# Sixteen more groups through the dense path of a one-core GNN attention kernel, and another order of the dense work within a batch

## The chip, the cores and the metric

One core of a Trainium2 chip runs the whole kernel. The metric is the device time in microseconds of one execution; three runs of the kernel before gave 3377.53 us in the median (3377.07 to 3377.69). The profile was taken in a separate execution that took 3376.22 us. A measurement of this kernel can tell a difference of about 0.2% from no change.

The engines are named as in the profile: PE is TensorE's matmul, PEld its weight load, DVE is VectorE, ACT is ScalarE, POOL is GpSimd and SP is SyncE, whose queue issues most DMAs.

## The reference, cut to what matters

12,500 nodes with 64 features; 400,000 edges with 64 features, sorted by destination. The density of the destinations falls with the node's number (they are drawn as 12500 u^2), so the first nodes have many edges each and the last ones few.

```python
h_src = nfeats[src]; h_dst = nfeats[dst]
e = leaky_relu(concat([h_src, h_dst, efeats]) @ W_attn + b_attn)[:, 0]
m = concat([h_src, efeats]) @ W_ne
alpha = segment softmax of e over dst
z = segment_sum(alpha[:, None] * m, dst)
out = relu(concat([nfeats, z]) @ W_out)
x = layernorm(x + out)
```

## The kernel before

Edges are cut into 782 groups of 512 (128 partitions by 4 places). There are two ways for a group.

**Gathered groups.** For each group four indirect DMAs on POOL (`gather`, L330) fetch 128 rows of 65 numbers from a table in DRAM: the node's score and its 64 features. 662 groups go this way, that is 2648 gathers. Sixteen groups make a batch and four make a part of a batch, so a batch has 64 gathers and four parts; there are 43 batches (numbered from 0), the last four of them smaller (10, 10, 12 and 6 groups, `ENDS`). A part gets its scores on DVE (`scores`, L373 to L391; the step L380 adds the gathered score and so waits for the gathers; ACT copies the window row and the edge rows first, L370 and L371). When all four parts have scores, a softmax over segments follows (`softmax`), which begins with the transpose L692 and ends with the transpose L754. It hops between DVE, ACT and PE four times: the first scan, line rows on PE (L596 `lines<-ident,bnd`), ends on one row, back to columns on PE (L599 `lines<-ident,line`), and the same again for the sums. The four gaps between these hops are filled by `dense_step(0)` to `dense_step(3)`. After the softmax the weights are made (L789), then PE multiplies the parts (L806): parts 0 and 1 at once, parts 2 and 3 ("later") in the gaps of the next batch's softmax. I call these products p0 to p3.

**Dense groups.** The first 120 groups, with the densest nodes, are not gathered. Each costs, spread over many batches:

- a *lookup* of its node scores: ACT makes a one-hot tile in a `big` buffer (L430, L431), PE multiplies it (L441), DVE picks the score (`look_scores`, L466 to L472). `look_rows` (L451 to L460) adds the edges' part, once a batch;
- after the softmax of its round (12 groups), a *count*: ACT makes four one-hot tiles (L480, L481) and one or two more where a group spans 6 or 7 nodes (L493, L494), DVE makes the weighted `lows` (L483), PE multiplies (L488, and L496 for the extra nodes), DVE adds the result into `counts` (`dense_sum`, L506, L509);
- *edge products* on PE (L549) and their sum on DVE (`edge_sum`, L558);
- per chunk of groups, a *node product* of `counts` with all node features: 25 matmuls on PE (L565). Then `node_pick` on DVE (L573, L576, and L578, which clears `counts`), `node_turn` on PE (L584) and `node_sum` on DVE (L590). I call a batch with a node product a node batch.

There are six `big` buffers, and each is free again only when PE has multiplied it. The dense groups are looked up and counted four per batch up to group 84 and three per batch beyond. Their chunks are 36, 12, 12, 8, 8, 8 groups and then six of 6, so that in the tail a node product comes with every second batch.

All engines run in the order in which the program is written (`manual_schedule`), each queue in order. In a batch the loop over its parts (i = 0 to 3) comes first, then the softmax with its steps. The order that the change touches is this one: within part 1 the first count (`dense_counts`) stands ahead of `between(k + 1)`, which prepares rows (`far`, `step`, `same`, `pen`, `mask`; L635 to L646) for the next softmax; `node_pick`, `edge_sum` and the first `look_scores` stand in `dense_step(0)`; the other counts of a batch stand at i = 2 (where four are to be counted) and in steps 2 and 3.

`BEHIND` ties some gathers of a batch (numbered 0 to 63) to PE's last instruction at named points of the batch before: gather 4 to the end of its parts ("counted"), 20, 24, 32 and 37 to its softmax steps 0 to 3, 44 and 49 to p0 and p1.

Of the kernel before, what the change touches and what calls it, by code (L numbers as in the profile page):

```python
# [15 lines left out]
P = 128  # L16
# [36 lines left out]
BEHIND = ((4, "counted"), (20, 0), (24, 1), (32, 2), (37, 3), (44, "first"), (49, "second"))  # L53
# [6 lines left out]
def sorted_path(ctx, tc, x, dst, idx, edge, w_ne, w_attn, b_attn, w_out, out, flag):  # L60
# [282 lines left out]
    def ahead_of(g0, n, b0):  # L343
# [7 lines left out]
        wrow = tiny.tile([P, SG, S], F32, name="wrow")[:, :, 0:Sk]  # L351
        for k in range(g0 // P, (g0 + n - 1) // P + 1):
            a, b1 = max(g0, k * P), min(g0 + n, (k + 1) * P)
            by = nc.sync if b0 > DG else nc.scalar
            by.dma_start(out=wrow[:, a - g0:b1 - g0, :],
                              in_=wins[k][a - k * P:b1 - k * P, 0:Sk].unsqueeze(0).to_broadcast([P, b1 - a, Sk]))
        fetched[g0] = ze, wrow
# [52 lines left out]
    def look_loads(g0, n):  # L410
# [3 lines left out]
        nc.sync.dma_start(out=wrow[:, 0:n], in_=wins[0][g0:g0 + n, 0:many].unsqueeze(0).to_broadcast([P, n, many]))  # L414
# [447 lines left out]
    ids = pre.tile([DG, P, 2 * T], I32, name="ids", bufs=1)  # L862
    nc.sync.dma_start(out=ids, in_=idx[0:DG])
# [10 lines left out]
    with before:  # L874
# [23 lines left out]
        with tc.manual_schedule(engines={EngineType.DVE, EngineType.Pool, EngineType.Activation, EngineType.PE, EngineType.SP}):  # L898
# [59 lines left out]
            parted_row = pre.tile([DG, P, T], I32, name="parted_row", bufs=1)  # L958
            nc.vector.tensor_scalar(parted_row, ids[:, :, 0:T], P - 1, None, op0=OP.bitwise_and)
            low_row = pre.tile([DG, P, T], BF16, name="low_row", bufs=1)  # L960
            nc.scalar.activation(low_row, parted_row, AF.Copy)
            nc.sync.dma_start(out=low_rows, in_=low_row)
# [147 lines left out]
    with loop:  # L1110
# [55 lines left out]
        with tc.manual_schedule(engines={EngineType.PE, EngineType.DVE, EngineType.Activation, EngineType.SP, EngineType.Pool}):  # L1166
# [14 lines left out]
            for k, G in enumerate(sizes):  # L1181
# [21 lines left out]
                after = None  # L1203
                for i, (g0, n) in enumerate(lots[k]):
# [39 lines left out]
                    if k and i in (1, 2):  # L1244
                        for g in batch_counts[i - 1:i] if i == 1 or len(batch_counts) > 3 else ():
# [15 lines left out]
                    if i == (0 if final else 1):  # L1261
                        if more:
# [574 lines left out]
```

## Time and profile before

| | |
|---|---|
| median of 3 runs | 3377.53 us |
| the profiled execution | 3376.22 us |
| its span, first to last instruction | 3374.5 us |
| PE / DVE / ACT / POOL busy | 2256.1 / 2131.6 / 1290.3 / 2512.3 us |
| gathers (L330) | 2648 |
| mean granted TensorE clock | 0.679 |

The timeline view has, per row: the start in us from the span's start, the length, the engine, the line and operation, what it writes and reads, how many such instructions were merged, and in brackets how long the engine had been idle and what ended the wait. The view of windows has, for each stretch, each engine's busy time, then the granted clock and the DMA share. In the view of groups the numbers behind the bar are the total busy time, the mean length in ns and the idle time ahead of the group.

### The profile page before, as it was taken

How to read it: one execution, taken by the hardware profiler on the slowest of the kernel's cores; microseconds unless marked ns; L12 is line 12 of the kernel's file. 1: busy time of each engine (PE TensorE's matmuls, PEld its weight loads, DVE VectorE, ACT ScalarE, POOL GpSimd, SP SyncE). 2: the span in 40 equal slices, each digit the busy share in tenths (PEclk: the TensorE clock that was granted, in tenths of full speed). 3: DMA queues.
4: the chain of work that ended last, by engine and by line, in shares of the span. 5: the costliest groups of instructions: out<-in, count | busy, mean ns of one | idle time of the engine just before them, and what ended most of it. 6: DMA issues, size and time to landing. Idle time of an engine off the chain costs nothing.

```text
span 3374.5 us, 38403 instructions
## 1 busy us (share of the span) xinstructions
PE 2256.1 (67%) x10066; PEld 1903.1 (56%) x10066; DVE 2131.6 (63%) x5517; ACT 1290.3 (38%) x2835; POOL 2512.3 (74%) x2676
## 2 busy tenths in 40 slices
PE   0244456677676787787778677756767787866764
PEld 0144446666665666575656565655656565655563
DVE  5644455566666676666676666656767676666666
ACT  1211123333343344444444444334454444544421
POOL 7777777777777777777777777777777777777773
PEclk9999985555555566666677676656767675766755
DMA  9333333333333333333333333333333333332331
GB/s 133 84 67 68 67 74 74 75 77 74 74 76 81 79 80 84 84 75 75 78 88 76 72 75 73 68 73 71 73 73 74 78 74 64 71 69 59 67 65 28
DMA packets 515059, 250.66 MB, mean 74 GB/s; under 512 B 351226, under 2 KB 472409, under 8 KB 514834
## 3 DMA queue, kind: packets, MB, share of 16 engines
q1 hardware_dynamic: 426588, 159.37, 20.3%
q0 software_dynamic: 84960, 88.33, 15.4%
q8 instruction: 86, 1.41, 0.2%
q10 hardware_dynamic: 3286, 0.40, 0.1%
q14 instruction: 139, 1.14, 0.1%
HBM read 241.09 MB, written 6.79 MB: 73 GB/s over the span
## 4 chain that ended last, share of the span: by engine, by line
PE 28%; POOL 27%; DVE 16%; issue 13%; DMA 11%; ACT 5%; DVEq 0%; POOLq 0%; ACTq 0%; SPq 0%
POOL zx L330 27%; PE pg L806 15%; DMA zx<-table,srcs 10%; PE pg L441 4%; PE pg L488 4%; DVE hot L382 1%; DVE pr L387 1%; DVE sdst L390 1%; DVE fixed L375 1%; DVE lows L483 1%; PE lines L596 1%; PE pg L565 1%; ACT big L480 1%; DVE pr L373 1%; DMA zx<-in_x_dram,srcs 1%
## 5 line engine op out<-in xcount | busy, mean ns | idle before, releaser
L330 POOL DMA_INDIRECT zx<-table,srcs x2584 | 2441.7, 945 | 787.5 <-issue 696.7
L806 PE MATMUL pg<-w,zx 128*128 128x16 f32 (+9 forms) x5152 | 1062.3, 379 | 14.2 <-DVE w L789 14.1
L806 PEld LDWEIGHTS pg<-w,zx 128*128 128x128 f32 x5152 | 1044.4, 313 | 34.9 <-DVE w L789 13.7
L488 PE MATMUL pg<-big,lows 128*128 128x490 f32 (+3 forms) x960 | 494.5, 679 | 212.9 <-DVE lows L483 201.9
L596 PE MATMUL lines<-ident,bnd 128*1 128x128 f32 x172 | 52.1, 406 | 763.7 <-ACT bnd L699 752.7
L488 PEld LDWEIGHTS pg<-big,lows 128*128 128x128 f32 x960 | 247.4, 272 | 399.1 <-issue 301.3
L596 PEld LDWEIGHTS lines<-ident,bnd 128*1 128x1 f32 x172 | 12.8, 97 | 784.7 <-ACT bnd L699 772.1
L480 ACT ACTIVATE big<-places,place 128x490 f32<-128x490 int16 (+3 forms) x480 | 294.0, 613 | 29.6 <-PE pg L441 28.9
L380 DVE TENSOR_TENSOR fixed<-fixed,zx 128x16 f32<-128x16 f32 (+3 forms) x172 | 31.7, 184 | 412.8 <-DMA zx<-table,srcs 408.7
L481 ACT ACTIVATE big<-big 128x490 f32<-128x490 f32 (+3 forms) x480 | 257.1, 536 | 15.3
L375 DVE TENSOR_REDUCE fixed<-pr 128x16 f32<-128x1024 f32 (+3 forms) x172 | 204.2, 1187 | 84.5 <-ACT fixed L370 73.7
L441 PE MATMUL pg<-s_src,big 128*128 128x98 f32 x960 | 257.5, 447 | 0.0
L441 PEld LDWEIGHTS pg<-s_src,big 128*128 128x128 f32 x960 | 235.6, 329 | 0.6
L370 ACT ACTIVATE fixed<-wrow 128x96 f32<-128x96 f32 (+11 forms) x172 | 45.1, 262 | 466.7 <-DVE w L789 136.2
L373 DVE TENSOR_TENSOR pr<-ze,lines 128x1024 f32<-128x1024 f32 (+3 forms) x172 | 201.2, 1170 | 2.0 <-DMA ze<-in_edge_dram 1.9
L694 ACT ACTIVATE soft<-turned 128x128 f32<-128x128 f32 x43 | 16.7, 388 | 465.6 <-DVE turned L692 465.6
L468 DVE TENSOR_TENSOR pr<-pr,pg 128x392 f32<-128x392 f32 x120 | 67.5, 563 | 198.0 <-PE pg L441 196.5
L371 ACT ACTIVATE zx<-ze 128x1024 f32<-128x1024 f32 (+3 forms) x172 | 176.5, 1026 | 5.9 <-issue 0.4
L825 DVE TENSOR_TENSOR acc<-acc,pg 128x16 f32 (+9 forms) x662 | 123.0, 186 | 82.1 <-issue 21.3
L483 DVE TENSOR_SCALAR lows<-fixed,low,kept 128x128 f32<-128x128 f32 x480 | 163.3, 401 | 3.5 <-PE pg L488 3.3
L565 PE MATMUL pg<-xall,counts 128*128 128x256 f32 x600 | 157.6, 429 | 0.6 <-DVE yo L1073 0.6
L506 DVE TENSOR_TENSOR counts<-counts,pg 128x490 f32 (+3 forms) x120 | 69.4, 578 | 137.8 <-PE pg L488 122.8
(303 smaller groups left out, 2792.0 us busy)
## 6 DMA issues: line engine op xcount, KB each, us to landing
ze<-in_edge_dram SPq DMA_DIRECT2D x157, 512.0 KB
zx<-table,srcs POOLq DMA_INDIRECT x2584
low_of<-low_rows SPq DMA_DIRECT2D x120, 128.0 KB
ep<-in_edge_dram SPq DMA_DIRECT2D x120, 128.0 KB
ed<-in_edge_dram SPq DMA_DIRECT2D x21, 512.0 KB
ed<-in_edge_dram SPq DMA_DIRECT2D x12, 384.0 KB
table<-xall SPq DMA_DIRECT2D x7, 455.0 KB
out_dram<-yo SPq DMA_DIRECT2D x24, 128.0 KB
```

Of the source, the lines that this page charges most:

```text
L330: row = nc.gpsimd.indirect_dma_start(out=zx[0:r, g, t, 1:EW] if plain else zx[0:r, g, t, 0:EW], out_offset=None, in_=x[:, :] if plain else ...
L371: nc.scalar.activation(zx[0:r, 0:n, :, EW:EW + D], ze[0:r, 0:n], AF.Copy)
L373: nc.vector.tensor_tensor(pr[0:r, 0:n], ze[0:r, 0:n], w_edge[0:r].unsqueeze(1).to_broadcast([r, n, T, D]), op=OP.mult)
L375: nc.vector.tensor_reduce(ysum[0:r, 0:n], pr[0:r, 0:n], axis=AX.X, op=OP.add)
L441: nc.tensor.matmul(found[:, t, :], hot[:, :, t], s_src, start=True, stop=True)
L480: nc.scalar.activation(hi, places[:, 0:wide], AF.Square, bias=place[:, t, g:g + 1])
L481: nc.scalar.activation(hi, hi, AF.Relu, scale=-1.0, bias=1.0)
L483: nc.vector.tensor_scalar(lows[t], count_, low[:, t, g:g + 1], kept[:, t, kept_at(g):kept_at(g) + 1], op0=OP.is_equal, op1=OP.mult)
L488: nc.tensor.matmul(to, lows[t], highs[t], start=(t == 0), stop=(t == T - 1))
L565: nc.tensor.matmul(pairs[0:m * ND, 0:m * D], counts[:, h0:h0 + m, :].rearrange("l h n -> l (h n)"), xall[:, h0:h0 + m, 1:EW], start=(h0 == ...
L806: nc.tensor.matmul(pg[:, g, :], zx[:, g, t, 1:EW + D], w[:, g, t, :], start=(t == 0), stop=(t == T - 1)).ins
L825: nc.vector.tensor_tensor(ag, ag, pg[:, g, :], op=OP.add)
```

## The change

Groups 120 to 135 become dense as well: 136 dense groups in 12 rounds, 646 gathered ones in 42 batches, 2584 gathers. All dense groups are now counted four per batch. From group 84 on a chunk is 4 groups, 13 times.

```diff
-ROUNDS = (12, 12, 12, 12, 12, 12, 12, 12, 12, 12)
+ROUNDS = (12, 12, 12, 12, 12, 12, 12, 12, 12, 12, 8, 8)
...
-EACHS = ((84, 4), (120, 3))
+EACHS = ((136, 4),)
...
-CHUNKS = ((36, 1), (12, 2), (8, 3), (6, 6))
-NODS = ((16, 2), (36, 3), (60, 4), (87, 5), (108, 6), (120, 7))
+CHUNKS = ((36, 1), (12, 2), (8, 3), (4, 13))
+NODS = ((16, 2), (36, 3), (60, 4), (84, 5), (108, 6), (136, 7))
...
-BEHIND = ((4, "counted"), (20, 0), (24, 1), (32, 2), (37, 3), (44, "first"), (49, "second"))
+BEHIND = ((20, 0), (24, 1), (32, 2), (37, 3), (44, "first"), (49, "second"))
...
+                    if k and i == 3:
+                        if opened:
+                            opened = node_pick(*opened)
+                            node_z = node_turn(*opened, shared)
+                        if summed:
+                            edge_sum(*summed)
+                            summed = None
+                        if seen:
+                            look_scores(*seen.pop(0))
+                        if chunk_of is None:
+                            for g in batch_counts[1:-1][-1:]:
+                                dense_sum(*open_counts.pop(0))
+                                open_counts.append(dense_counts(g))
+                                while len(open_counts) > 1:
+                                    dense_sum(*open_counts.pop(0))
                     hot = scores(g0, n, tiles[i], drel, b0, k == 0)
...
+                    if i == (0 if final else 1):
+                        if more:
+                            as_floats(k + 2, lists[k + 2])
+                        if k + 1 < len(sizes):
+                            after = between(k + 1)
                     parts.append((g0, n, tiles[i], hot))
...
-                        for g in batch_counts[i - 1:i] if i == 1 or len(batch_counts) > 3 else ():
+                        for g in batch_counts[i - 1:i] if i == 1 or (len(batch_counts) > 3 and chunk_of is None) else ():
...
-                    if n == 0 and opened:
-                        opened = node_pick(*opened)
-                    if n == 0 and summed:
-                        edge_sum(*summed)
-                        summed = None
+                    if n == 0 and node_z:
+                        node_sum(*node_z)
...
-                    if n in (0, 3):
+                    if n in (0, 2, 3):
...
-                    if n > 1:
-                        for g in batch_counts[-2:-1] if n == 2 and len(batch_counts) > 2 else batch_counts[1:][-1:] if n == 3 else ():
-                            open_counts.append(dense_counts(g))
+                    inner = batch_counts[1:] if chunk_of is not None else batch_counts[1:][-1:]
+                    for g in inner[n - 4:][:1] if len(inner) >= 4 - n > 0 else ():
+                        open_counts.append(dense_counts(g))
```

Besides, the table of indices of the dense groups (`ids`) is loaded and converted in three pieces of 64 groups instead of one of 120 ahead of the first batch, through one buffer, and the window rows (`wrow`) are broadcast as whole rows of 48.

In a batch with a node product three of the four counts now stand in the softmax, in steps 1, 2 and 3; in one without, one stands at each of the parts 1, 2 and 3 and one in step 3.

The first place is PE in the softmax of a node batch near the end of the lookups, from the first return to columns (L599) to the second. In these rows `bnd` is what goes to a line, `line` what comes back; L806 are products of a later part, L441 a lookup, L488 and L496 a count. Before (batch 32; the other batches with counts have the same sequence there, with or without a node product):

```order
L599 MATMUL lines<-ident,line 128x1 x2
L801 MATMUL pg<-zx,ident 1x4x8
L806 MATMUL pg<-w,zx 128x40 x8
L441 MATMUL pg<-s_src,big 128x98 x4
L596 MATMUL lines<-ident,bnd 1x4x32 x2
L806 MATMUL pg<-w,zx 128x40 x8
L488 MATMUL pg<-big,lows 128x490 x4
L496 MATMUL pps<-big,lows 128x98 x4
L599 MATMUL lines<-ident,line 128x1 x2
```

and in the changed kernel (batch 30):

```order
L599 MATMUL lines<-ident,line 128x1 x2
L801 MATMUL pg<-zx,ident 1x4x8
L806 MATMUL pg<-w,zx 128x40 x8
L441 MATMUL pg<-s_src,big 128x98 x4
L488 MATMUL pg<-big,lows 128x490 x4
L496 MATMUL pps<-big,lows 128x98 x4
L596 MATMUL lines<-ident,bnd 1x4x32 x2
L806 MATMUL pg<-w,zx 128x40 x8
L441 MATMUL pg<-s_src,big 128x98 x4
L488 MATMUL pg<-big,lows 128x490 x4
L496 MATMUL pps<-big,lows 128x98 x4
L599 MATMUL lines<-ident,line 128x1 x2
```

A count has come in ahead of the line rows L596, and a fourth lookup ahead of the second count.

The second place is DVE around the scores of the last part of a node batch. L387 to L391 are the end of these scores, L692 begins the softmax; `pr<-pg,own`, `sums_` and `counts` are `node_pick`, `acce` is the edge sum. Before (batch 33):

```order
L387 TENSOR_TENSOR pr<-hot,fixed 128x16x40
L390 TENSOR_REDUCE sdst<-pr 128x16
L391 TENSOR_TENSOR soft<-fixed,sdst 128x4x4
L692 STREAM_TRANSPOSE turned<-soft 128x128
L695 SCALAR_TENSOR_TENSOR soft<-turned,soft 128x128
L696 SCALAR_TENSOR_TENSOR soft<-step,soft 128x128
L697 SCALAR_TENSOR_TENSOR soft<-step,soft 128x128
L573 TENSOR_TENSOR pr<-pg,own 128x256
L576 TENSOR_REDUCE sums__19594<-pr 128x64
L578 MEMSET counts 128x3136
```

and in the changed kernel (batch 31), with L460 the last row of `look_rows` and L373 the first of the last part's scores:

```order
L460 TENSOR_TENSOR y_dense<-total 128x4x4
L573 TENSOR_TENSOR pr<-pg,own 128x256
L576 TENSOR_REDUCE sums__19063<-pr 128x64
L578 MEMSET counts 128x3136
L532 TENSOR_LOAD dn
L558 ISA
L558 TENSOR_TENSOR acce<-acce,pg 64x6
...
L466 TENSOR_TENSOR pr<-fixed,high 128x392
L468 TENSOR_TENSOR pr<-pr,pg 128x392
L470 TENSOR_REDUCE picked<-pr 128x4
L472 TENSOR_TENSOR y_dense<-y_dense,picked 128x4
L373 TENSOR_TENSOR pr<-ze,lines 128x1024
```

The pick, the edge sums and the first lookup's score have moved from behind L697, inside the softmax, to ahead of the last part's scores.

The third place is ACT between the copies for part 1 and those for part 2 of a node batch. `far` belongs to `between`, L493 and L494 to the extra nodes of the first count, `fixed<-wrow` (L370) is the copy that the next part's scores need. Before (batch 33):

```order
L480 ACTIVATE big<-places,place 128x490
L481 ACTIVATE big<-big 128x490
L493 ACTIVATE big<-places,place 128x98 x4
L494 ACTIVATE big<-big 128x392
L286 ACTIVATE lines<-srcs 128x64
L635 ACTIVATE far<-edges_of_75 128x130
...
L646 ACTIVATE mask<-pen 128x256
L370 ACTIVATE fixed<-wrow 128x4x40
```

and in the changed kernel (batch 31):

```order
L286 ACTIVATE lines<-srcs 128x64
L635 ACTIVATE far<-edges_of_75 128x130
...
L646 ACTIVATE mask<-pen 128x256
L430 ACTIVATE big<-low_of,p_col 128x512
L431 ACTIVATE big<-big 128x512
...
L493 ACTIVATE big<-places,place 128x98 x4
L494 ACTIVATE big<-big 128x392
L370 ACTIVATE fixed<-wrow 128x4x40
```

The rows for the next softmax now stand ahead of the count, and the copy for part 2 stands directly behind it.

In the changed kernel PE has the node product L565 in batches 14, 17, 20, 22, 24 and in every batch from 26 to 39; before it had it in 14, 17, 20, 22, 24, 26, 29, 31, 33, 35, 37 and 39. Lookups reach up to batch 34 and counts up to batch 38, which is now the first of the four short batches; before, the short batches 39 to 42 had no counts.

More of the change, by code (lines that the diff above doesn't have):

```diff
@@ L350, in ahead_of @@
         ze = early.pop(g0) if g0 in early else edges(g0, n)
-        wrow = tiny.tile([P, SG, S], F32, name="wrow")[:, :, 0:Sk]
+        wrow = tiny.tile([P, SG, S], F32, name="wrow")
         for k in range(g0 // P, (g0 + n - 1) // P + 1):
@@ L861, in sorted_path @@
     lists[1] = listed(1)
-    ids = pre.tile([DG, P, 2 * T], I32, name="ids", bufs=1)
-    nc.sync.dma_start(out=ids, in_=idx[0:DG])
+    thirds = [(a, min(a + P // 2, DG)) for a in range(0, DG, P // 2)]
+    ids_parts = []
+    for a, b in thirds:
+        ids = pre.tile([P // 2, P, 2 * T], I32, name="ids", bufs=1)
+        ids_parts.append(ids)
+        if a == 0:
+            nc.sync.dma_start(out=ids[0:b - a], in_=idx[a:b])
     nc.sync.dma_start(out=meet, in_=dst[DG * GE - 1:DG * GE + 1].unsqueeze(0))
@@ L1202, in sorted_path @@
                 parts = []
-                after = None
+                after = node_z = None
                 for i, (g0, n) in enumerate(lots[k]):
```

39 lines of the change are left out of this document (16 added, 23 removed).

## The prediction

> **What bounds the kernel now.** I read the groups by line first, then the timeline of POOL, then the batches' starts (the transpose L692 on DVE), then one late node batch engine by engine.
>
> ```profile
> L330 POOL DMA_INDIRECT zx<-table,srcs x2584 | 2441.7, 945 | 787.5 <-issue 696.7 <-DMA zx<-table,srcs 55.8 <-PE pg L488 5.5
> 2737.93 0.95 POOL L330 DMA_INDIRECT zx<-table,srcs  x1 [0.30 <-issue]
> 181.82 0.18 DVE L380 TENSOR_TENSOR fixed<-fixed,zx 128x16 f32<-128x16 f32 x1 [12.68 <-DMA zx<-table,srcs]
> 2982.45 0.32 DVE L692 STREAM_TRANSPOSE turned<-soft 128x128 f32<-128x128 f32 x1
> 3059.06 0.18 DVE L380 TENSOR_TENSOR fixed<-fixed,zx 128x16 f32<-128x16 f32 x1 [8.18 <-DMA zx<-table,srcs]
> 3062.26 0.32 DVE L692 STREAM_TRANSPOSE turned<-soft 128x128 f32<-128x128 f32 x1
> ```
>
> A gather with the pause ahead of it takes (2441.7 + 787.5) / 2584 = 1.25 us, so 64 take 79.9 us. The pause is 0.30 us and almost all "issue": POOL waits for nothing, and PE's ties held it by 5.5 us in all, mostly not beyond that pause. So the gathers are the clock of the kernel. Batch 36 to 37 takes 79.8 us from L692 to L692, and DVE spends 8.2 us of it waiting for the last part's gathers: the chain of DVE, ACT and PE alone would need 71.6 us. That wait is the reserve of a batch.
>
> The reserve is not everywhere. This is batch 32 to 33, a late node batch with three lookups and three counts:
>
> ```profile
> 2662.40 0.32 DVE L692 STREAM_TRANSPOSE turned<-soft 128x128 f32<-128x128 f32 x1
> 2729.38 0.29 DVE L639 CUSTOM_DVE_ANT_0 step<-far 128x129 f32<-128x129 f32 x1 [7.20 <-ACT far L635]
> 2731.28 1.23 DVE L375 TENSOR_REDUCE fixed<-pr 128x16 f32<-128x1024 f32 x1 [0.47 <-ACT fixed L370]
> 2740.94 0.18 DVE L380 TENSOR_TENSOR fixed<-fixed,zx 128x16 f32<-128x16 f32 x1
> 2743.94 0.32 DVE L692 STREAM_TRANSPOSE turned<-soft 128x128 f32<-128x128 f32 x1
> ```
>
> It takes 81.5 us, and the last part's L380 (2740.94) has no wait at all. Here the chain is already longer than the gathers. The chain's inside, PE and ACT:
>
> ```profile
> 2672.28 2.15 PE L441 MATMUL pg<-s_src,big 128*128 128x98 f32 x8
> 2680.22 0.64 PE L596 MATMUL lines<-ident,bnd 128*1 128x128 f32 x2
> 2680.65 3.48 PE L806 MATMUL pg<-w,zx 128*128 128x40 f32 x16
> 2683.92 5.48 PE L488 MATMUL pg<-big,lows 128*128 128x490 f32 x8
> 2689.24 1.03 PE L496 MATMUL pps<-big,lows 128*128 128x98 f32 x8
> 2692.23 3.52 PE L488 MATMUL pg<-big,lows 128*128 128x490 f32 x8 [1.75 <-ACT big L494]
> 2698.89 4.69 PE L806 MATMUL pg<-w,zx 128*128 128x40 f32 x32
> 2703.70 7.05 PE L806 MATMUL pg<-w,zx 128*128 128x40 f32 x32
> 2710.55 13.24 PE L565 MATMUL pg<-xall,counts 128*128 128x256 f32 x50
> 2727.20 1.18 ACT L493 ACTIVATE big<-places,place 128x98 f32<-128x98 int16 x4 [6.42 <-PE pg L441]
> 2730.96 0.29 ACT L370 ACTIVATE fixed<-wrow 128x160 f32<-128x160 f32 x1
> ```
>
> The softmax's line rows stand in PE's queue behind lookups and counts, so each of these in front of a line row lengthens the softmax. After it come p0, p1, the node product, the edges and the first lookup; ACT's L493 waits 6.4 us for the `big` buffer which that lookup frees, and DVE waits behind ACT.
>
> **The change, part by part.** I work against the profiled execution (span 3374.5, time 3376.2 us, 1.3 below the median).
>
> *The gathers.* 64 fewer at 1.25 us: -79.9 us, wherever they are the clock. This is one batch.
>
> *Batches 1 to 25.* With waits like the 8.2 and 12.7 us above, I cost the new order at nothing: a single node batch grows by the block of 7.5 us below, and the wait at its last part takes that in. If the cover falls short, I put it at 2 us for each of the five node batches there. The pieces of `ids` queue two more rounds of load, convert and store on SP, DVE and ACT ahead of batch 0. No row shows their price; whatever it is up to 12.7 us, batch 1's wait in the row 181.82 takes it in. The whole-row `wrow` copies I cost at nothing either: they are issued a part ahead.
>
> *A late node batch with four lookups (26 to 34).* Before, such a batch came every second time; now it comes every time, with one more lookup and one more count. I start from the 81.5 us above.
>
> 1. Softmax. A count stands ahead of L596: +5.48 + 1.03 = 6.5. A lookup stands ahead of the next L599: +2.15. Against that, the second count follows a first one and finds the faster clock: 3.52 instead of 5.48, and the half part ahead of it 1.8 instead of 3.48 (by the clock rows below). Sum +5.0 (3.5 to 7).
> 2. The block ahead of the last part. Its price is in step 0 of batch 33:
>
> ```profile
> 2745.92 0.41 DVE L573 TENSOR_TENSOR pr<-pg,own 128x256 f32<-128x256 f32 x1
> 2747.55 2.67 DVE L578 MEMSET counts<- 128x3136 f32 x1 [0.60 <-issue]
> 2752.80 0.17 DVE L472 TENSOR_TENSOR y_dense<-y_dense,picked 128x4 f32<-128x4 f32 x1
> 2665.44 7.05 PE L806 MATMUL pg<-w,zx 128*128 128x40 f32 x32
> 2753.95 0.42 PE L584 MATMUL pg<-node,sums__19594 128*64 128x32 f32 x2
> 2756.42 0.37 PE L599 MATMUL lines<-ident,line 1*128 1x1 f32 x2
> 2674.36 0.37 PE L599 MATMUL lines<-ident,line 1*128 1x1 f32 x2
> ```
>
> From 2745.92 to 2752.97 is 7.05 us, and a fourth group's edge sum about 0.5 more: +7.5. In step 0 it cost nearly nothing, because PE is busy there with 7.05 us of p2 and 2.15 of a lookup: the line rows L599 come 12.5 us after L692 with the block (2756.42) and 12.0 without it (2674.36). Ahead of the last part it is hidden only by a wait for gathers, and here there is none. What was free is now paid in full.
> 3. `between` ahead of the count. The 7.20 us wait at L639 goes, but what is late next is the copy L370 for part 2: it stands behind L493, and L493 still waits for the lookup behind the node product. L375 moves from 2731.28 to just behind L493, L494 and L370, at about 2729.2: -2.0, not -7.2.
> 4. A fourth group in the edge products, `look_rows` and weights: +0.5, +0.7, +0.35.
>
> 81.5 + 5.0 + 7.5 - 2.0 + 1.5 = 93.5 us against 79.9: 13.6 us late in each batch. From batch 32 on the groups have seven nodes: 0.9 more for each of two counts in the softmax, and one more L493 and L494 ahead of L370 (1.7): +3.5, 97. POOL feels it through its ties. Gather 32 comes 40 us after a batch's first one; step 2, to which it is tied, would end some 33 us after L692, and L692 follows the last gather by 4 us at least. So after some 3 us of lateness POOL waits as well, and the batch's length is the chain's.
>
> *Late node batches without lookups (35 to 37).* Chain 71.6; a count in step 1:
>
> ```profile
> 3000.08 6.11 PE L488 MATMUL pg<-big,lows 128*128 128x490 f32 x8
> 3006.03 1.92 PE L496 MATMUL pps<-big,lows 128*128 128x98 f32 x16
> ```
>
> 6.11 + 1.92 = 8.0, minus 2.6 for the next count and 1.7 for the half part, plus a wait of that next count for its tiles, 1.8 as in the row 2692.23: +5.5. Pick and edge sums, from L573 to where the lookup's score began in step 0, and a fourth edge sum: 7.5 less the 2 us of the score, +5.6. The rest -0.4. Sum 82.3 us.
>
> *The sum over batches 25 to 37.* 25 to 26 has the block, but a softmax that loses its middle count and gains a lookup: 81.5 - 4.4 + 7.5 - 2.0 + 1.5 = 84.1. 34 to 35 has the long softmax, but no lookups after it:
>
> ```profile
> 2695.14 0.33 DVE L754 STREAM_TRANSPOSE fixed<-turned 128x128 f32<-128x128 f32 x1
> 3013.22 0.33 DVE L754 STREAM_TRANSPOSE fixed<-turned 128x128 f32<-128x128 f32 x1
> ```
>
> The softmax of batch 32 took 32.7 us and that of batch 36 30.8, so 71.6 + (32.7 + 5.0 + 1.8 - 30.8) + 5.6 - 0.4 = 85.5. With six of 93.5, two of 97 and two of 82.3 this is 1089 us. Twelve times 79.9 is 959: +130 us.
>
> *The short batches.*
>
> ```profile
> 3142.23 0.32 DVE L692 STREAM_TRANSPOSE turned<-soft 128x128 f32<-128x128 f32 x1
> 3202.99 0.24 DVE L692 STREAM_TRANSPOSE turned<-soft 128x128 f32<-128x128 f32 x1
> ```
>
> From 3142.23 to the span's end is 232.3 us. The first of them, 3142.23 to 3202.99, had its last part at no wait either. Now four counts fall into a batch with only 40 gathers: softmax of batch 37 +5.5; pick and edge sums of batch 38 +7.8, the 5.6 and about 2 of waiting for the node product; softmax of batch 38 +16, a slow and a fast count (8.0 + 5.5) and 2.5 for the `lows` and the sum of a third; batch 39's pick and edge sums, again behind a node product that a short batch has little to cover with, +5.5. Sum +35 (20 to 40).
>
> Total: -79.9 + 130 + 35 = +85; 3376.2 + 85 + 1.3, to the median's level, = **3463 us**.
>
> [...] The granted clock decides the length of the products:
>
> ```profile
> 2665.30:2672.30 7.00, 7.00 (x36) 6.89 (x35) 4.06 (x12) 1.90 (x3) 5.28 (x6) 0.50 0.16 27
> 2723.70:2732.00 8.30, 7.64 (x37) 5.69 (x36) 2.15 (x4) 4.46 (x14) 6.17 (x8) 1.00 0.15 24
> 3017.86 3.77 PE L806 MATMUL pg<-w,zx 128*128 128x44 f32 x32
> ```
>
> At 0.50 a part takes 7.05 us, right behind wide counts 3.77. [...]
>
> **The rivals.**
>
> *The block stays hidden (faster, 0.10).* DVE still waits for the gathers at the last part, so the pick costs nothing and the chain fits 79.9 us. For it: the waits of 8.18 and 12.68 us. Against it: batch 32 to 33 has none. Time: 3377.5 - 79.9 + 35 = 3333, 3298 if the short batches hide theirs too. It decides for this if the chain with lookups stays under 80 us.
>
> *PE runs at full clock through the late batches (0.11).* Then p2 saves 3.3 us, the half part 1.7, p0 0.9 and p1 3.3: 9.2 per batch. 93.5 becomes 84.3 and 97 becomes 87.8, the others fall to the gathers' pace: 6 x 4.4 + 2 x 7.9 = 42, and one batch's 9 off the short batches' 35. 3377.5 - 79.9 + 42 + 26 = 3366. For it: the clock is higher where node products are; against it: the rows above. [...]
>
> *More stalls than that (slower still, 0.05).* Each of the five earlier node batches loses 2 us as well, and the later ones 98 instead of 93.5: 3463 + 10 + 36 = 3509.
>
> **How the numbers follow.** My case has 0.74: slower, 3463, by itself 3410 (batches of 88 instead of 93.5) to 3505 (of 98). The bound of 0.2%, about what a measurement of this kernel can tell from no change, is 6.8 us; the second rival lies near it, mostly on the faster side. Faster 0.17, same 0.03, slower 0.80. The range goes from 3360 to 3505 and leaves out the first rival, half of the second and the third.
>
> **What would show it.** Right: POOL at 1.25 us per gather up to batch 25, then gaps released by PE; L692 to L692 near 93 us from batch 26 to 34 and near 82 after; no wait at the last part's L380; part 2's L375 waiting for ACT's L370. Wrong: a wait for gathers at the last part in batches 27 to 33, or L806 at 3.8 us in step 0.

## The result and the profile after

The changed kernel takes 3470.48 us (median of 4 runs, 3469.5 to 3474.35), the kernel before 3377.61 in the same comparison: a ratio of 1.0277, 95% interval 1.026 to 1.0295. The profiled execution took 3470.18 us, its span is 3468.4.

These are the groups by line of the changed kernel (busy time and mean ns of one, then the idle time ahead of them with its releaser), and below them the last two in the kernel before:

```profile
L330 POOL DMA_INDIRECT zx<-table,srcs x2520 | 2378.6, 944 | 936.4 <-issue 701.7 <-PE lines L596 74.3 <-PE pg L441 50.2
L375 DVE TENSOR_REDUCE fixed<-pr 128x16 f32<-128x1024 f32 (+2 forms) x168 | 199.3, 1186 | 152.5 <-ACT fixed L370 138.6
L380 DVE TENSOR_TENSOR fixed<-fixed,zx 128x16 f32<-128x16 f32 (+2 forms) x168 | 30.9, 184 | 211.0 <-DMA zx<-table,srcs 206.6
```

```profile
L375 DVE TENSOR_REDUCE fixed<-pr 128x16 f32<-128x1024 f32 (+3 forms) x172 | 204.2, 1187 | 84.5 <-ACT fixed L370 73.7
L380 DVE TENSOR_TENSOR fixed<-fixed,zx 128x16 f32<-128x16 f32 (+3 forms) x172 | 31.7, 184 | 412.8 <-DMA zx<-table,srcs 408.7
```

The gathers are 64 fewer and each is as fast as before (944 ns in the mean, 945 before), but POOL's idle time grew from 787.5 to 936.4 us, and most of the new part is released by PE (74.3 and 50.2): POOL waits for the batch now. DVE's wait for gathers fell from 408.7 to 206.6 us, its wait for ACT's copy L370 rose from 73.7 to 138.6. Up to batch 25 almost nothing is lost. These are the starts of the softmaxes (L692 on DVE) of batches 25, 26, 32, 34, 35 and 37:

```profile
2103.17 0.32 DVE L692 STREAM_TRANSPOSE turned<-soft 128x128 f32<-128x128 f32 x1
2187.86 0.32 DVE L692 STREAM_TRANSPOSE turned<-soft 128x128 f32<-128x128 f32 x1
2740.80 0.32 DVE L692 STREAM_TRANSPOSE turned<-soft 128x128 f32<-128x128 f32 x1
2933.08 0.32 DVE L692 STREAM_TRANSPOSE turned<-soft 128x128 f32<-128x128 f32 x1
3023.75 0.32 DVE L692 STREAM_TRANSPOSE turned<-soft 128x128 f32<-128x128 f32 x1
3197.89 0.32 DVE L692 STREAM_TRANSPOSE turned<-soft 128x128 f32<-128x128 f32 x1
```

Batch 25 starts 0.4 us later than before (2102.75). From 26 to 32 a batch takes (2740.80 - 2187.86) / 6 = 92.2 us, from 32 to 34 it takes 96.1, then 90.7, and 87.1 from 35 to 37. Behind 3197.89 there are 270.5 us to the end of the span.

Inside such a stretch, from the softmax of batch 28 to the end of that of batch 29, the timeline of DVE answers to the rows of batch 32 before:

```profile
2372.44 0.32 DVE L692 STREAM_TRANSPOSE turned<-soft 128x128 f32<-128x128 f32 x1
...
2445.42 1.23 DVE L375 TENSOR_REDUCE fixed<-pr 128x16 f32<-128x1024 f32 x1 [4.40 <-ACT fixed L370]
...
2453.07 0.42 DVE L573 TENSOR_TENSOR pr<-pg,own 128x256 f32<-128x256 f32 x1
...
2459.95 0.17 DVE L472 TENSOR_TENSOR y_dense<-y_dense,picked 128x4 f32<-128x4 f32 x1
...
2462.96 0.18 DVE L380 TENSOR_TENSOR fixed<-fixed,zx 128x16 f32<-128x16 f32 x1
...
2465.97 0.32 DVE L692 STREAM_TRANSPOSE turned<-soft 128x128 f32<-128x128 f32 x1
...
2503.12 0.33 DVE L754 STREAM_TRANSPOSE fixed<-turned 128x128 f32<-128x128 f32 x1
```

The block from L573 to L472 takes 7.05 us, the last part's L380 behind it has no wait for gathers, and part 2's L375 waits 4.40 us for ACT. The softmax of batch 29 takes 37.2 us from L692 to L754; the mean of batches 26 to 31 is 37.8. POOL shows the lateness through two ties (its timeline, the idle time in front):

```profile
2384.74 0.94 POOL L330 DMA_INDIRECT zx<-table,srcs  x1 [6.06 <-PE pg L441]
2396.21 0.94 POOL L330 DMA_INDIRECT zx<-table,srcs  x1 [6.78 <-PE lines L596]
```

These are gathers 20 and 24, tied to steps 0 and 1: 12.8 us together, nearly the 13.6 by which this stretch of 93.5 us exceeds 79.9. It is the batch that is long; the ties pass that on.

PE shows the clock in the same softmax. The first row is p2 in step 0, the second its window (after POOL's count come the granted clock and the DMA):

```profile
2469.01 7.04 PE L806 MATMUL pg<-w,zx 128*128 128x36 f32 x32
2469.00:2476.00 7.00, 7.00 (x35) 6.99 (x33) 1.55 (x5) 5.65 (x10) 1.73 (x2) 0.50 0.32 42
```

### The profile page after: what moved, and what is told of

It reads as the page before. It is cut to its first block, busy times and chain, and to the rows that moved or that the text cites. A ratio compares the mean times of both kernels' runs of the same rounds, so it can differ in the third digit from the quotient of the medians.

```text
span 3468.4 us, 40639 instructions
## 1 busy us (share of the span) xinstructions
PE 2384.2 (69%) x10885; PEld 1990.9 (57%) x10885; DVE 2221.7 (64%) x5719; ACT 1442.9 (42%) x3159; POOL 2449.1 (71%) x2612
## 5 line engine op out<-in xcount | busy, mean ns | idle before, releaser
L330 POOL DMA_INDIRECT zx<-table,srcs x2520 | 2378.6, 944 | 936.4 <-issue 701.7
L806 PE MATMUL pg<-w,zx 128*128 128x40 f32 (+9 forms) x5024 | 992.6, 368 | 13.5 <-DVE w L789 13.5
L806 PEld LDWEIGHTS pg<-w,zx 128*128 128x128 f32 x5024 | 973.7, 301 | 32.3 <-DVE w L789 12.7
L488 PE MATMUL pg<-big,lows 128*128 128x490 f32 (+3 forms) x1088 | 548.9, 666 | 268.0 <-DVE lows L483 264.4
L488 PEld LDWEIGHTS pg<-big,lows 128*128 128x128 f32 x1088 | 270.5, 262 | 479.6 <-issue 326.3
L596 PE MATMUL lines<-ident,bnd 128*1 128x128 f32 x168 | 46.4, 374 | 612.6 <-ACT bnd L699 568.1
L596 PEld LDWEIGHTS lines<-ident,bnd 128*1 128x1 f32 x168 | 11.6, 90 | 630.3 <-ACT bnd L699 615.7
L375 DVE TENSOR_REDUCE fixed<-pr 128x16 f32<-128x1024 f32 (+2 forms) x168 | 199.3, 1186 | 152.5 <-ACT fixed L370 138.6
L441 PE MATMUL pg<-s_src,big 128*128 128x98 f32 x1088 | 289.9, 438 | 0.0
L441 PEld LDWEIGHTS pg<-s_src,big 128*128 128x128 f32 x1088 | 266.8, 330 | 0.0
L370 ACT ACTIVATE fixed<-wrow 128x80 f32<-128x80 f32 (+9 forms) x168 | 44.2, 263 | 522.4 <-DVE w L789 161.9
L565 PE MATMUL pg<-xall,counts 128*128 128x256 f32 x950 | 248.4, 428 | 3.8 <-DVE yo L1082 3.8
L565 PEld LDWEIGHTS pg<-xall,counts 128*128 128x128 f32 x950 | 204.8, 220 | 44.5 <-issue 7.9
L373 DVE TENSOR_TENSOR pr<-ze,lines 128x1024 f32<-128x1024 f32 (+2 forms) x168 | 196.4, 1169 | 2.3 <-DMA ze<-in_edge_dram 2.1
L371 ACT ACTIVATE zx<-ze 128x1024 f32<-128x1024 f32 (+2 forms) x168 | 172.3, 1026 | 6.3 <-issue 0.7
L825 DVE TENSOR_TENSOR acc<-acc,pg 128x28 f32 (+9 forms) x646 | 120.4, 186 | 80.9 <-issue 24.8
L380 DVE TENSOR_TENSOR fixed<-fixed,zx 128x16 f32<-128x16 f32 (+2 forms) x168 | 30.9, 184 | 211.0 <-DMA zx<-table,srcs 206.6
L506 DVE TENSOR_TENSOR counts<-counts,pg 128x490 f32 (+3 forms) x136 | 79.9, 588 | 113.3 <-PE pg L488 99.8
```

The costliest lines, as they stand in the source:

```text
L330: row = nc.gpsimd.indirect_dma_start(out=zx[0:r, g, t, 1:EW] if plain else zx[0:r, g, t, 0:EW], out_offset=None, in_=x[:, :] if plain else ...
L371: nc.scalar.activation(zx[0:r, 0:n, :, EW:EW + D], ze[0:r, 0:n], AF.Copy)
L373: nc.vector.tensor_tensor(pr[0:r, 0:n], ze[0:r, 0:n], w_edge[0:r].unsqueeze(1).to_broadcast([r, n, T, D]), op=OP.mult)
L375: nc.vector.tensor_reduce(ysum[0:r, 0:n], pr[0:r, 0:n], axis=AX.X, op=OP.add)
L441: nc.tensor.matmul(found[:, t, :], hot[:, :, t], s_src, start=True, stop=True)
L488: nc.tensor.matmul(to, lows[t], highs[t], start=(t == 0), stop=(t == T - 1))
```

## The experiments

**e1: the block back in step 0.** The pick, the memset, the edge sum and the first lookup's score stand in the softmax's step 0 again in node batches (with them `node_turn` moves to the end of step 0 and `node_sum` to step 1):

```diff
                     if k and i == 3:
-                        if opened:
-                            opened = node_pick(*opened)
-                            node_z = node_turn(*opened, shared)
-                        if summed:
-                            edge_sum(*summed)
...
                 def dense_work(n):
+                    if n == 0 and opened:
+                        opened = node_pick(*opened)
+                    if n == 0 and summed:
+                        edge_sum(*summed)
```

> The changed kernel, but in node batches the pick, the memset, the edge sum and the first lookup's score stand in step 0 of the softmax again, as before the change; 136 groups, the rows of the next softmax ahead of the count and the count in step 1 stay. Theory (the block ahead of the last part is paid in full, and step 0 hides it behind 7 us of p2): the nine lengths from batch 25 to 34 fall by 7 to 7.5 us each from about 92.5 to 85, those of batches 34 to 38 by 5 to 6, the softmax stays near 38.4 us: 3470 - 65 - 22 = 3385 us (3370 to 3405). Rival 'the block was hidden anyway' (PE or ACT is the bound ahead of the last part): 3470, no change. Rival 'step 0 has no room any more, since a count is queued in step 1': the softmax grows by what the block takes, 3455 to 3470.

Measured: 3400.51 us, 1.0058 (1.0041 to 1.0075) of the kernel before. The rows of DVE at the start of batches 26 and 32, and part 2's wait between them:

```profile
2189.28 0.32 DVE L692 STREAM_TRANSPOSE turned<-soft 128x128 f32<-128x128 f32 x1
...
2433.55 1.23 DVE L375 TENSOR_REDUCE fixed<-pr 128x16 f32<-128x1024 f32 x1 [4.34 <-ACT fixed L370]
...
2703.64 0.32 DVE L692 STREAM_TRANSPOSE turned<-soft 128x128 f32<-128x128 f32 x1
```

A batch takes 85.7 us, 6.4 less than in the changed kernel, with the same wait for ACT as in the changed kernel. From part 2's L375 to the next softmax a batch takes 13.1 us instead of 20.1, the mean of batches 26 to 31: 7.0 less, which is the block, so the rival by which it was hidden falls. The nine lengths from 25 to 34 fall by 54 us together for the 65 expected, those from 34 to 38 by 16 for 22. Less comes back from batch 32 on, where the groups have seven nodes: there the softmax is longer than in the changed kernel (41.4 against 38.7 us in batch 32). Batch 25 itself started some 8 us later in this run, 4.6 of them from a longer start-up.

**e2: the copies for part 2 ahead of the first count.** One move on ACT's queue; the rest is the changed kernel:

```diff
+                    if k and i == 1 and batch_counts and not final:
+                        copies(*lots[k][2], tiles[2], b0)
                     if k and i in (1, 2):
...
```

`copies` is the two activations L370 and L371, taken out of `scores`, which skips them where they have been issued.

> The changed kernel, with one more move: ACT's copies L370 and L371 for part 2 are issued ahead of the first count instead of behind it. In the changed kernel DVE waits 4.40 us at part 2's L375 (2445.42) for L370, which stands behind ten activations of the count. The recorded step says that L493's wait for `big` is what holds it; in the changed kernel's trace L493 waits 0.18 us only (2443.45), so ACT's own queue is the rival cause. Queue theory: the wait at L375 goes, 4.2 us in each of nine late lookup batches and 2 to 4 in the four behind them: 3470 - 38 - 10 = 3422 us (3412 to 3435), and nothing becomes later, since the count's sum is wanted in step 0 only. If the node product and the lookup on PE are the real bound of that stretch, the last part's block waits for them instead and the time stays within 10 us of 3470.

Measured: 3401.54 us, 1.0067 (1.005 to 1.0084). Starts of batches 26 and 32 on DVE, and the group of the same reduction (L387 in this kernel):

```profile
2188.11 0.32 DVE L704 STREAM_TRANSPOSE turned<-soft 128x128 f32<-128x128 f32 x1
...
2702.78 0.32 DVE L704 STREAM_TRANSPOSE turned<-soft 128x128 f32<-128x128 f32 x1
```

```profile
L387 DVE TENSOR_REDUCE fixed<-pr 128x16 f32<-128x1024 f32 (+2 forms) x168 | 199.3, 1186 | 65.0 <-ACT fixed L373 52.2
```

A batch takes 85.8 us, again 6.4 less: more than the 4.2 that I had read from one batch, and the total lies below the range expected. The wait for the copies falls from 138.6 to 52.2 us. What held ACT is in two rows of the changed kernel, in batches 28 and 26, with DVE's wait behind the second:

```profile
2443.45 1.18 ACT L493 ACTIVATE big<-places,place 128x98 f32<-128x98 int16 x4 [0.18 <-PE pg L441]
...
2258.18 1.18 ACT L493 ACTIVATE big<-places,place 128x98 f32<-128x98 int16 x4 [6.88 <-PE pg L441]
2260.13 1.23 DVE L375 TENSOR_REDUCE fixed<-pr 128x16 f32<-128x1024 f32 x1 [10.82 <-ACT fixed L370]
```

In three of the batches 26 to 31 the wait for the `big` buffer is there (6.88, 2.46 and 4.60 us); in the other three it is under 0.7, and the copies are simply behind the count's own activations. Part 2's wait in those six is 10.82, 6.70, 4.40, 4.57, 8.53 and 5.78 us, 6.8 in the mean.

**e3: the order alone.** The changed order with the tables of before:

```diff
-ROUNDS = (12, 12, 12, 12, 12, 12, 12, 12, 12, 12, 8, 8)
+ROUNDS = (12, 12, 12, 12, 12, 12, 12, 12, 12, 12)
-EACHS = ((136, 4),)
+EACHS = ((84, 4), (120, 3))
-CHUNKS = ((36, 1), (12, 2), (8, 3), (4, 13))
+CHUNKS = ((36, 1), (12, 2), (8, 3), (6, 6))
```

with `NODS` as before the change.

> The changed kernel's order of work with the tables of before (120 dense groups, lots of 3 behind group 84, chunks of 6). Theory (each late batch needs the block, the fourth lookup and count and the node product together to exceed the gathers' pace): a node batch grows by 7.5 - 2.0 = 5.5 us, its last part's wait was 2.6, 0.0 and 0.1 us in the three that matter, and the batches between them have waits of 4.9 to 9 us that give it back; some 3 us each are lost through the ties, and about 6 in the short batches: 3377.5 + 9 + 6 = 3393 us (3380 to 3410). Rival 'the order alone makes most of the loss': above 3430. Rival 'the order is free or better, the 16 groups make the loss': 3370 to 3378.

Measured: 3377.47 us, 0.9993 (0.9983 to 1.0002): no difference, so my 3393 was wrong and the rival "the order is free" holds. The softmax of batch 30 on DVE in this kernel, and then in the kernel before:

```profile
2507.69 0.32 DVE L692 STREAM_TRANSPOSE turned<-soft 128x128 f32<-128x128 f32 x1
2532.57 0.33 DVE L754 STREAM_TRANSPOSE fixed<-turned 128x128 f32<-128x128 f32 x1
```

```profile
2502.67 0.32 DVE L692 STREAM_TRANSPOSE turned<-soft 128x128 f32<-128x128 f32 x1
2535.05 0.33 DVE L754 STREAM_TRANSPOSE fixed<-turned 128x128 f32<-128x128 f32 x1
```

24.9 us against 32.4. In a batch without node products the new order takes the middle count out of the softmax and puts it ahead of the last part. As I read it, that gives back in the one batch what the block costs in the other. With 136 groups every late batch is a node batch, and there is no such other batch. So the order alone makes no loss. The pieces of `ids` and the whole rows of `wrow` are in this kernel too, so they cost nothing that shows. 136 groups in the order of before were not run: what the groups alone would have cost is not shown, only that 136 groups can win (e10 below).

**e4: wide products kept up.** The first count's L488 products issued six times over, in the gap of PE ahead of the softmax:

```diff
-        for t in range(T):
+        for t in list(range(T)) * times:
             nc.tensor.matmul(to, lows[t], highs[t], start=(t == 0), stop=(t == T - 1))
```

> The changed kernel, but from batch 26 on the first count of a node batch issues its L488 products six times over instead of once (each repetition starts the sum anew, so the result is the same): 5 times 3.5 us = 17.4 us more wide products in the 20 us in which PE is idle ahead of the softmax (from 2447.6 to 2468.3). It tells what the granted clock is worth. Clock theory (wide products keep the clock up for some us; p2's 7.04 us in step 0 and the half part's 3.63 are lengths at clock 0.50, and the softmax waits for them): p2 takes 3.7 us, the half part 1.9, the softmax shortens from 38.4 to 33 us: 3470 - 9 x 5 - 4 x 4 = 3410 us (3395 to 3430). If the clock falls back at once with the narrow products, or the softmax waits for ACT and DVE rather than PE: 3465 to 3475. If the extra products get in front of the transposes L596 of the softmax: slower, up to 3500.

Measured: 3624.39 us, 1.0719 (1.0701 to 1.0737). None of the three times expected. The row of DVE in step with the block:

```profile
2495.99 0.15 DVE L558 TENSOR_TENSOR acce<-acce,pg 64x6 f32 x1 [7.79 <-PE pg L584]
```

The block's own matmul L584 stood behind the repeats, and the edge sum waited for it. PE was then idle for 12 us before the softmax, and p2 took 7.04 us as before. As a test of the clock it says nothing; it only made the batch longer (102.8 us in the mean of 26 to 31 instead of 92.2).

**e7: the repeats behind L584.** Three repeats only, issued at the last part behind the block's matmul:

```diff
+                    if i == 3 and chunk_of is not None and k > 25 and batch_counts:
+                        to, lows, highs = products_of
+                        for t in list(range(T)) * 3:
+                            nc.tensor.matmul(to, lows[t], highs[t], start=(t == 0), stop=(t == T - 1))
```

> The changed kernel with the first count's L488 products issued three times more, but now behind the matmul L584 of the block and right ahead of the softmax's transposes (in e4 L584 stood behind them and the edge sum waited 7.79 us for it, and PE was idle for 12.07 us between the wide products and p2). Same result, more PE work in a gap of 13.7 us. Clock theory: p2 (7.04 us in step 0) takes about 3.7 us, the half part 1.9 to 2.5, the softmax 33 to 34 instead of 38.4: 3470 - 9 x 4.5 - 4 x 4 = 3413 us (3400 to 3430). If the clock falls with the narrow products themselves: p2 still above 6 us and 3465 to 3480. If the repeats end behind ACT's `bnd`: up to 1 us later per batch, 3483.

This run, with e5, e6, e8 and e9, fell on a chip where every kernel took far longer, and e11 and e12 fell on another such chip (the kernel before took 4085 to 4108 us there). On the first of them PE stood still for "issue" (339.5 us ahead of the edge products in e5, 314.8 in e6); only stretches in which PE has no such gap are used from the runs on both. The time was 4715.14 us, 1.1548 (1.1499 to 1.1597) of the kernel before there, which tells nothing of the clock. Its PE rows in batch 28's softmax are whole, with the two windows behind them (the granted clock is the number after POOL's count):

```profile
3150.63 12.24 PE L1252 MATMUL pg<-big,lows 128*128 128x490 f32 x24
...
3164.46 3.76 PE L809 MATMUL pg<-w,zx 128*128 128x36 f32 x32
...
3170.64 3.63 PE L809 MATMUL pg<-w,zx 128*128 128x36 f32 x16
```

```profile
3164.00:3171.00 7.00, 6.95 (x50) 6.34 (x48) 2.94 (x9) 4.74 (x8) 0.51 (x1) 0.83 0.24 30
3171.00:3176.00 5.00, 5.00 (x24) 5.00 (x24) 4.09 (x14) 4.72 (x15) 3.27 (x4) 0.50 0.18 24
```

p2 takes 3.76 us instead of 7.04, and the granted clock from 3164 to 3171 is 0.83 instead of 0.50: here it was still up in step 0. But the half part 6 us later is back at 3.63 us and clock 0.50, though PE was busy for 11.95 of the 12 us of the two windows. Batch 28 is one of the two best: in batches 26 to 31 p2 took between 3.76 and 6.76 us, 5.1 in the mean. The second `bnd` transposes stand 21.2 us behind the transpose of the scores in the mean, instead of 23.4 in the changed kernel: about what p2 saved (2.0) arrives there. The whole softmax did not get shorter (37.9 us against 37.8 in the mean), on another chip; what a fast p2 is worth to the kernel stays open, and the half part, p0 and p1 were not made fast at all.

**e6: without the count in step 1** (one group's count in four is left out from batch 25 on).

```diff
-                    for g in inner[n - 4:][:1] if len(inner) >= 4 - n > 0 else ():
+                    for g in inner[n - 4:][:1] if len(inner) >= 4 - n > 0 and not (n == 1 and k > 24) else ():
```

> The changed kernel without the count in step 1 from batch 25 on: one of four groups' counts is left out there, so the node sums lack it. It prices the recorded step 'a count ahead of L596, 6.5 us less what the faster clock gives back: +5.0'. Theory (the second transposes L596 stand behind that count in PE's queue): the softmax shortens from 38.4 to 33 us in the nine late lookup batches and by 5 in the four behind them: 3470 - 9 x 5 - 4 x 5 = 3405 us (3390 to 3425). Rival (the softmax waits for DVE's and ACT's own chain, the count runs beside it): 3460 to 3475.

> The kernel of e6 on another chip: the changed kernel without the count in step 1 from batch 25 on (one of four groups' counts is left out there, so the node sums lack it). In e6 the softmax took 35.6 us instead of 38.4, which is the record's 6.5 less 1.96 and 1.7. Theory: the count's net price is 2.8 us in each of nine late lookup batches and 1 to 4 in four behind them: 3470 - 25 - 10 = 3435 us (3420 to 3450), a ratio of 1.012 to 1.022 to the kernel before. Rival, by the gross price (6.5 us of PE time, wherever it stands): 3470 - 13 x 6.5 = 3385, 1.002.

The runs fell on the two disturbed chips: 4643.12 us, 1.1378 (1.1328 to 1.1429), and 4622.88, 1.1278 (1.1245 to 1.1311). The totals tell nothing. The softmax of batch 28 in e6:

```profile
3131.61 0.32 DVE L692 STREAM_TRANSPOSE turned<-soft 128x128 f32<-128x128 f32 x1
3166.92 0.33 DVE L754 STREAM_TRANSPOSE fixed<-turned 128x128 f32<-128x128 f32 x1
```

35.3 us; over batches 26 to 31 it is 2.5 us shorter in the mean than in the changed kernel (e11 on its chip: 2.3). The net price in the prediction was 6.5 - 1.96 - 1.7 = 2.84. The size agrees, but one part of it does not: the count that follows takes 4.81 us in e6 and 4.84 in the changed kernel, in the mean, so it gains nothing from the count ahead of it. The half part does (1.87 us instead of 3.47). What that gives in the kernel's time stays unmeasured.

**e5, e9, e10: block and copies together.** The edits of e1 and e2 in one kernel.

> The edits of e1 and e2 together: block in step 0, copies of part 2 ahead of the first count; 136 groups. Alone they took 6.4 us each from the mean batch of 26 to 32 (92.2 to 85.7 and 85.8), and the excess over the gathers' pace of 79.9 is 12.3. If both stand on one serial chain (block and copies one after the other on DVE, the theory), their gains add: batches of 80 to 82 us, 25 to 34 in about 725 us, 34 to 38 in 322, some 190 behind that: 3340 us (3325 to 3365), faster than both kernels. Rival: each of them uncovers the same next bound (PE's p0, p1, node product and lookup one after the other, or the softmax): batches stay at 84 to 85 and the time at 3380 to 3395.

> The kernel of e5 and e9 once more, in the hope of a chip whose engines are not held by 'issue'. Block in step 0 and copies of part 2 ahead of the first count; 136 groups. Serial chain (theory): the gains of e1 and e2 add, batches of 80 to 82 us from 26 on, 3340 us (3325 to 3365), a ratio of 0.985 to 0.997 to the kernel before. Rival: each uncovers the same next bound: batches of 84 to 85, 3380 to 3395, a ratio of 1.00 to 1.005.

e5 and e9, the same kernel, fell on the first disturbed chip: 4441.92 us, 1.085 (1.0783 to 1.0918), and 4454.46, 1.0868 (1.0797 to 1.094). e10 did not: **3342.7 us, 0.9871 (0.9855 to 0.9888)** of the kernel before on its chip, and far below the changed kernel's 3470.48, which was not run there. Starts of batches 26, 32 and 37, and the last part's wait of batch 28 (L392 is L380 here):

```profile
2188.12 0.32 DVE L704 STREAM_TRANSPOSE turned<-soft 128x128 f32<-128x128 f32 x1
...
2345.49 0.18 DVE L392 TENSOR_TENSOR fixed<-fixed,zx 128x16 f32<-128x16 f32 x1 [1.01 <-DMA zx<-table,srcs]
...
2671.83 0.32 DVE L704 STREAM_TRANSPOSE turned<-soft 128x128 f32<-128x128 f32 x1
...
3082.91 0.32 DVE L704 STREAM_TRANSPOSE turned<-soft 128x128 f32<-128x128 f32 x1
```

A batch takes 80.6 us. In three of the six batches the last part waits for a gather again (5.53, 1.01 and 4.59 us), in the others, of 80.4 to 82.0 us, it does not: both gains add, down to about the gathers' pace. So block and copies stood on one serial chain, and no other bound lay between 86 and 80.6. From batch 32 to 34 the batches are still 82 to 85 us.

**e8, e12: the same with 128 dense groups.**

```diff
-ROUNDS = (12, 12, 12, 12, 12, 12, 12, 12, 12, 12, 8, 8)
+ROUNDS = (12, 12, 12, 12, 12, 12, 12, 12, 12, 12, 8)
-EACHS = ((136, 4),)
+EACHS = ((128, 4),)
```

with two chunks of four fewer.

> e5 with 128 dense groups instead of 136 (two chunks of 4 fewer, 32 gathers more, a first batch of 8 groups). The recorded step on the short batches says that four counts a batch that run into batches with 40 gathers cost 20 to 40 us. Theory: the gathers cost 32 x 1.25 = 40 us more, and the dense work ends half a batch earlier, which gives 10 to 30 back: e5 + 10 to 30, 3350 to 3375 us. If the short batches' cost has nothing to do with where the dense work ends: e5 + 40, about 3380. If the late batches with four counts are still over the gathers' pace in e5, each that is gone gives that back as well: below e5 + 10.

> The kernel of e8 on another chip: e10 with 128 dense groups instead of 136. In e10 the span from batch 37's softmax to the end is 26 us longer than the same stretch before, and late batches from 28 on are 0.2 to 5 us over the gathers' pace. The recorded step puts the short batches' cost down to dense work that runs into batches with 40 gathers. Theory: 40 us more of gathers, the dense work ends half a batch earlier and gives 10 to 30 back: 3342 + 10 to 30, 3350 to 3372 us, 0.990 to 0.996 of the kernel before. If the short batches' cost does not hang on the dense work: 3342 + 40 = 3382, 0.999.

One on each of the disturbed chips: 4489.85 us, 1.0983 (1.0933 to 1.1032), and 4421.16, 1.0769 (1.0741 to 1.0797). They decide nothing: whether the short batches' cost goes when the dense work ends earlier stays open.

## Why the prediction was right, step by step

- **Gathers, 1.25 us each.** Right: up to batch 25 the batches keep the gathers' pace in sum, and batch 25 starts at 2103.17.
- **Batches 1 to 25 free.** Right in sum. The lengths from batches 20, 22 and 24 were 81.8, 83.9 and 83.0 us, longer than the wait at the last part could take in; the batches behind 20 and 22 gave most of that back. From batch 1 to 25 it comes to 2.8 us, and batch 1 started 2.4 earlier.
- **Late batches with lookups, 93.5 us.** 92.2 from 26 to 32. The softmax was put at 32.7 + 5.0 = 37.7, and the mean of batches 26 to 31 is 37.8. Inside this sum one term failed: "the second count follows a first one and finds the faster clock: 3.52 instead of 5.48" (the granted clock in these two rows of the kernel before was 1.00 and 0.64). It took 4.84 us in the mean, and the first one 4.87 instead of 5.48; that the two errors mostly cancel is luck. The block was put at 7.5; its rows show 7.05, e1 takes 7.0 out where it stood, and 6.4 of that reach the batch. The +1.5 of step 4 does not show apart.
- **"-2.0, since L493 still waits for the lookup".** The size held: part 2's L375 starts 72.0 us behind L692 in the mean of the six batches, 66.9 without the growth of the softmax, and it started at 68.9 in batch 32 before. The cause held only by half: in three of six batches it is that buffer, in the others ACT's own queue. DVE's wait at L639 was replaced by 6.8 us at L375, as the step said of what is late next. That it could be had by moving two copies I did not see.
- **97 us from 32 to 34.** 96.1. **25 to 26, 84.1:** 84.7.
- **34 to 35, 85.5, and 82.3 behind it.** 90.7 and 87.1 (84.5 and 89.7): too low by 5. The step "the rest -0.4" failed. It left out the copies' wait, which is in the batches without lookups as well, while at L639 there was only 0.74 us to gain (batch 36 before). These are part 2's L375 in the three stretches from 34 to 37, and then the starts of batches 34 and 37 in e2, where the copies stand first:

```profile
3008.49 1.23 DVE L375 TENSOR_REDUCE fixed<-pr 128x16 f32<-128x1024 f32 x1 [4.39 <-ACT fixed L370]
3092.97 1.23 DVE L375 TENSOR_REDUCE fixed<-pr 128x16 f32<-128x1024 f32 x1 [4.14 <-ACT fixed L370]
3182.64 1.23 DVE L375 TENSOR_REDUCE fixed<-pr 128x16 f32<-128x1024 f32 x1 [4.41 <-ACT fixed L370]
```

```profile
2879.73 0.32 DVE L704 STREAM_TRANSPOSE turned<-soft 128x128 f32<-128x128 f32 x1
3131.59 0.32 DVE L704 STREAM_TRANSPOSE turned<-soft 128x128 f32<-128x128 f32 x1
```

  The three batches take 264.8 us in the changed kernel and 251.9 in e2, 12.9 less, which is the sum of the three waits; the prediction had 250.1. In batches 34 and 36 DVE also waits 2.00 and 3.66 us behind the softmax (L761, for PE's L599), a term that the sum does not have, and the three softmaxes came out 1.4, 2.2 and 1.7 us below the sum's; these nearly cancel. What makes L599 late there is not shown.
- **Sum 25 to 37.** 1094.7 us against 1089.
- **The short batches, +35.** 270.5 us behind the start of batch 37's softmax against 232.3: +38. In e10 it is 3341.2 - 3082.91 = 258.3, so 12 of the 38 are block and copies. Most of the other 26 is in the first two softmaxes, in which counts stand now. The first one's end and the second one's start and end, in the changed kernel:

```profile
3231.88 0.33 DVE L754 STREAM_TRANSPOSE fixed<-turned 128x128 f32<-128x128 f32 x1
3276.59 0.24 DVE L692 STREAM_TRANSPOSE turned<-soft 128x128 f32<-128x128 f32 x1
3310.45 0.33 DVE L754 STREAM_TRANSPOSE fixed<-turned 128x128 f32<-128x128 f32 x1
```

  They grew from 29.4 to 34.0 and from 20.3 to 33.9 us (before, they ended at 3171.62 and 3223.30), 18.2 together, where the prediction had 5.5 + 16; in e10 they take 34.7 and 34.8. That the counts are what lengthens them is argued: no run that can be used took them out.
- **Where POOL waits.** The ties hold it, but at gathers 20 and 24, not from 32 on.
- **The sum.** 3463 against 3470 is closer than its terms: the six batches at 93.5 were 8 us too high together, the three behind 34's start 15 us too low, the short batches 3 too low. The bounds of the range do not come out of its text either: eight batches of 88 or of 98 instead of 93.5 give 3419 and 3499, not 3410 and 3505.
- **The first rival** falls by e1 and by the last part's L380, which has no wait. **The third** falls: the early batches lost 2.8 us for its 10, and the later ones stayed below 98.
- **The second rival (full clock).** p2 at 7.04 us and clock 0.50 speak against it in the changed kernel, with PE busy for all of that window's 7.00 us. The two lengths that its price rests on are there in the kernel before: a part took 7.05 us at clock 0.50 (2703.80 to 2710.50) and 3.77 at clock 1.00 (3017.90 to 3021.60). That a PE without gaps would stay at the higher clock, no run shows: in e7 it was at 0.50 from 3171 on, in a stretch in which it was busy for 11.95 of 12 us. The rival's price of 9.2 us a batch was not tested: e7 made only p2 fast, and not in every batch.

## What to carry to other kernels

Work that is free where an engine waits has a price as soon as the wait is gone, so before more work is put into a batch, read its reserve at the wait that ends last, and read it in every kind of batch: here the new order cost nothing with 120 groups, and with 136 the kernel was 2.8% slower. When a chain is serial, look on the feeding engine for two short instructions that stand behind a long block for no reason; here moving them was worth as much as moving the block, 6.4 us a batch each. A tuned place (step 0 of the softmax, behind 7 us of products) is known by what hides it, not by what stands next to it.

## What was not expected of the hardware

On the first of the two chips on which every kernel took far longer, PE stood still for "issue" in code that has no such gaps in the changed kernel. In e7's PE timeline single node products follow each other at 2.1 to 2.8 us, where 50 of them take 12.77 us in the changed kernel's batch 28:

```profile
3106.26 0.59 PE L568 MATMUL pg<-xall,counts 128*128 128x256 f32 x1 [2.21 <-issue]
3108.36 0.58 PE L568 MATMUL pg<-xall,counts 128*128 128x256 f32 x1 [1.51 <-issue]
```

In e5 PE's edge products alone waited 339.5 us in this way; in the changed kernel, on an undisturbed chip, they wait 0.0 us, and PE's waits for "issue" come to 1.1 us in all. On this first chip the kernel before lost 21% (4085 against 3378 us), e10's kernel 33% (4442 against 3343), so that the order of the two turned round. The gathers themselves were not slower (944 ns each in e5). What held the instructions back no run shows, nor what made the kernel before take 4108 us on the second chip; a comparison holds for the chip on which it was made.
